# Two graph-attention layers on one core: gather buffers from a list of free ones, an earlier fetch at the change of layers, a moved transpose, the last tile by halves

## The chip, the cores and the metric

The kernel runs on one core of one Trainium2 chip. The metric is the device time of one execution in microseconds (us). The time before is the median of three runs, 1907.87 us (1905.23, 1907.87 and 1914.99).

## The reference

x is 3327 x 1024 in float32, adj is a symmetric 0/1 matrix with ones on its diagonal, in which an off-diagonal entry is set with a chance of about 0.0048. Cut to what matters:

```python
def layer0(x, adj, W, a_src, a_dst):          # 8 heads of 128
    h = (x @ W).reshape(C, H, D)
    e = leaky_relu(alpha_src[:, :, None] + alpha_dst[:, None, :], 0.2)
    attn = softmax(where(adj == 0, -inf, e), axis=-1)
    return einsum('hij,hjd->hid', attn, h)    # heads side by side

def layer1(x, adj, W, a1, a2):                # one head
    h = x @ W
    e = leaky_relu(h @ a1 + (h @ a2).T, 0.2)
    return relu(softmax(where(adj > 0, e, NEG), axis=1) @ h)

x = layernorm(x + layer0(x, adj, ...))
x = layernorm(x + layer1(x, adj, ...))
```

## The kernel before

The rows are cut into NT = 26 tiles of 128 (the last one has 127). A first stage projects x with layer 0's weights, one tile after the other, writes the projected rows to a table h0_d in DRAM, and works out for every tile the lists of its neighbours. It also sums layer 0's first half of sources for the first 13 tiles (the "early" ones). What is in question here comes after it, in the function `sparse`.

There a tile's neighbours are laid out in blocks. A tile of layer 1 ("Target") has blocks 0 to 4: four of 4 x 128 rows and a last one of 128 rows, the end. In layer 0 a late tile has the same five blocks, an early tile only 2, 3 and 4. For each block the function `gather` fetches the neighbours' rows from the table with indirect DMAs issued on POOL (L1034), four for a block, one for an end. A row of the table is 4.2 KB in layer 0 (h0_d) and 4.1 KB in layer 1 (y_d), so that a block is some 2.1 MB. The buffers are five for blocks (two named `near`, three `src`) and two for ends; they are taken round and round, a ring. A fetch goes out when the tenant before, five blocks back in the order of fetches, has been summed (`send`, L1320).

With a block in SBUF, `weights` works out its attention weights on DVE with a hand-over to ACT (layer 0: L1110, L1111, ACT's copy L1113, and e, L1115; layer 1: L1246, L1247, L1249), and `sums` multiplies it by PE into PSUM (L1146 in layer 0, L1258 in layer 1). `own` (L1080 on, L1224 on) adds the tile's own row. What is left of an item, its `finish`, is a generator that is advanced a step at a time while the following items run:

- Layer 0: the denominators (DVE met L1168, PE den L1169); dividing and adding x (L1172 to L1178); layer norm (L218 to L225) and two score products (L1185); three exponentials on ACT (L1190 to L1192, the last is `grow`) and the store of the row tile into y_d (L1193); last a transpose of `grow` on PE (L1197), its copy to a line on ACT (L1199) and the store of that line (L1200).
- Layer 1: transposing the sum z (L197, L200), multiplying it with layer 1's weights (L1290, 2 x 8 matmuls), ReLU and residual (L1293), layer norm, store (L1301).

The order of the instructions on every engine is the order in which the Python code emits them; nothing reorders them afterwards. `rest(i, n)` says how: before the first block of item i (n = 0) and after each block (n = 1 on) it advances the finishes of earlier items by the plan of the item's kind. In a pair such as (2, 1) the first number is an item two back, the second the item before. The plan of a layer 0 item with five blocks is

```python
len(Target.blocks): ((2,), (1,), (1,), (1,), (1,), (1,)),
```

so the last step of a finish (L1197, L1199, L1200) is emitted ahead of the first block's sums of the item two later, right after the exponentials of L1190 to L1192 and ahead of `own`.

Where the layers change, layer 1's gathers read y_d. Blocks 0 and 1 need only the first 13 tiles of it (`ready`, L1209), blocks 2 to 4 all 26. The list of fetches therefore goes, with A, B, C for targets 0, 1, 2: A0 A1 B0 B1, then A2 A3 A4 B2 B3 B4, then C0 and so on in order. The last item of layer 0 is finished in one go there (L1353), its row tile is stored, and A2 can be fetched.

Of the kernel before, what the change touches and what calls it, by code (L numbers as in the profile page):

```python
# [13 lines left out]
AF = mybir.ActivationFunctionType  # L14
OP = mybir.AluOpType
# [4 lines left out]
P = 128  # L20
SLOPE = 0.2
EPS = 1e-5
# [4 lines left out]
def kernel(  # L27
# [28 lines left out]
    nc = tc.nc  # L56
    N, D = x.shape
    H, DH = a0_src.shape
    NT = (N + P - 1) // P
# [4 lines left out]
    HALF = 512  # L64
    CT = 4
# [5 lines left out]
    EB = 4  # L71
    NB = NG * EB + 1
    WD = NP // 8
    HW0 = D + 2 * H
    HW = D + 4
# [6 lines left out]
    HB = EB // 2  # L82
# [31 lines left out]
    h0_d = scratch.tile([NP, HP], F32, name="h0_d")  # L114
    y_d = scratch.tile([NP, HP], F32, name="y_d")
# [19 lines left out]
    near = [const.tile([P, NG, HG], F32, name=f"near{b}") for b in range(HB)]  # L135
# [37 lines left out]
    class Phase:  # L173
# [16 lines left out]
        def sbuf(self, tag, shape, bufs, name=None, dt=F32):  # L190
            return self.pool.tile(shape, dt, tag=tag, name=name or tag, bufs=bufs)
# [322 lines left out]
    with ExitStack() as own, tc.manual_schedule():  # L514
        ph = Phase(own, "proj", {"A": 2, "T": 1})
# [243 lines left out]
        for n in range(4):  # L759
            half = slice(n % 2 * HALF, (n % 2 + 1) * HALF)  # L760
# [62 lines left out]
        for g in range(NG):  # L823
            nc.vector.memset(tri[g * GT : (g + 1) * GT, g * GT : (g + 1) * GT], 1.0)
        nc.gpsimd.affine_select(
            out=tri, in_=tri, pattern=[[1, P]], compare_op=OP.is_ge, fill=0.0, base=0, channel_multiplier=-1
# [7 lines left out]
            out=tri, in_=tri, pattern=[[1, P]], compare_op=OP.is_ge, fill=0.0, base=0, channel_multiplier=-1  # L834
# [35 lines left out]
        for t in range(3, NT):  # L870
# [3 lines left out]
            if t == 12:  # L874
                n, own_a = NT - 1, pool.tile([P, NT], I32, bufs=1, name="own")
# [95 lines left out]
    def sparse(own):  # L971
        ph = Phase(own, "sparse", {"A": 4, "S": 2, "T": 1, "E": 1})
        pool, bank, sbuf = ph.pool, ph.bank, ph.sbuf
        NS = 5
        srcs = near + [pool.tile([P, NG, HG], F32, bufs=1, name=f"src{n}") for n in range(HB, NS)]
        ends = [pool.tile([P, 1, HG], F32, bufs=1, name=f"end{n}") for n in range(2)]
# [46 lines left out]
        listed = {}  # L1023
        reach = {THR: nc.gpsimd.to_reg(THR - 1), NP: nc.gpsimd.to_reg(NP - 1)}
        stored = set()
        taken = [[(0, b) for b in range(HB)], []]

        def gather(table, w, t, b):
            end, n = b == EB, THR if b < HB else NP
            ring = ends if end else srcs  # L1030
            s = ring[len(taken[end]) % len(ring)]
            taken[end].append(None)
            for g in range(NG if b < EB else 1):
                nc.gpsimd.indirect_dma_start(  # L1034
                    out=s[:, g, :w], out_offset=None, in_=table[:n, :],
                    in_offset=bass.IndirectOffsetOnAxis(ap=idx[:, t, b * NG + g : b * NG + g + 1], axis=0),
                    bounds_check=reach[n], oob_is_err=False,
                )
            return s

        def get_edges(t):
            listed[t] = sbuf("re", [P, NB, H], 3)
# [14 lines left out]
        class Layer0:  # L1057


            def __init__(self, t, n):  # L1060
                self.t, self.n, self.src, self.made = t, n, {}, {}
                self.blocks = tuple(range(HB if t < EARLY else 0, EB + 1))

            def ready(self, b):
# [33 lines left out]
                self.acc = [bank("A", [P, 4, DH], "acc") for _ in range(2)]  # L1098

            def fetch(self, b):  # L1100
                self.src[b] = gather(h0_d, HW0, self.t, b)

            def weights(self, b):

# [97 lines left out]
        class Target:  # L1202
# [1 line left out]
            blocks = tuple(range(EB + 1))  # L1204

            def __init__(self, t, n):
                self.t, self.n, self.src, self.made = t, n, {}, {}

            def ready(self, b):  # L1209
                return stored.issuperset(range(NTH if b < HB else NT))  # L1210
# [20 lines left out]
                nc.vector.tensor_tensor(es[:, :1], es[:, 1:], loop[:, t : t + 1], OP.mult)  # L1231

            def fetch(self, b):
                self.src[b] = gather(y_d, HW, self.t, b)

            def begin(self):
                self.acc = {c: bank("A", [P, CUTS[1]], "acc1") for c in (2, 0, 1)}
# [42 lines left out]
            def finish(self):  # L1280

                t, z, res = self.t, self.z, self.res
                xT = sbuf("xT", [P, KT, P], 2)
                yield from ph.transposed(xT, z, (0, 1))
                o = sbuf("z", [P, D], 3, "o")
                for g in range(2):
                    half = slice(g * HALF, (g + 1) * HALF)
                    acc = bank("S", [P, HALF], "mm")
                    for k in range(KT):
                        nc.tensor.matmul(acc, xT[:, k, :], wt1[:, k, half], start=k == 0, stop=k == KT - 1)  # L1290
                        if k in (1, 3, 5):
                            yield
                    nc.vector.scalar_tensor_tensor(o[:, half], acc, 0.0, res[:, half], op0=OP.max, op1=OP.add)  # L1293
                    if g == 1:
                        ahead.append(self.settle(o))
                    yield

            def settle(self, o):
                yield from ph.norm_steps([o])
                for r in pieces(self.t):  # L1300
                    nc.sync.dma_start(out[at(self.t, r), :], o[r])  # L1301

        def pipeline(items, fetches):

            left, sums_of, sent = [], set(), [0]
            plans = {
                len(Target.blocks): ((2,), (1,), (1,), (1,), (1,), (1,)),
                len(Target.blocks) - HB: ((2,), (1, 1), (1, 1), (1,)),
                Target: ((2,), (2, 1), (2, 1), (1, 1), (1, 1), (1,)),
            }  # L1310

            def rest(i, n):
                it = items[i] if i < len(items) else items[-1]
                plan = plans[Target] if isinstance(it, Target) else plans[len(it.blocks)]
                for who in plan[n]:
                    k = i - who
                    if 0 <= k < len(left):
                        next(left[k], None)

            def send():  # L1320
                while sent[0] < len(fetches):
                    i, b = fetches[sent[0]]
                    end = b == EB
                    ring = len(ends) if end else NS
                    held = taken[end][-ring:]
                    if len(held) == ring and held[0] not in sums_of or not items[i].ready(b):
                        return
                    items[i].fetch(b)
                    taken[end][-1] = (i, b)
                    sent[0] += 1  # L1330

            def get(i):
                if i < len(items) and isinstance(items[i], Layer0):
                    get_edges(items[i].t)

            get(0)
            items[0].prepare()
            for av, a in zip(avs, (a1_src, a1_dst)):
                spread(av, a)
            for b in range(HB):  # L1340
                items[0].src[b] = near[b]
            send()
            items[0].weights(items[0].blocks[0])
            for i, it in enumerate(items):
                after = items[i + 1] if i + 1 < len(items) else None
                turn = isinstance(it, Target) and isinstance(items[i - 1], Layer0)
                it.begin()
                nb = len(it.blocks)
                for j, b in enumerate(it.blocks):
                    if j == 0 and i:  # L1350
                        items[i - 1].close()
                        if turn:
                            for _ in range(5):  # L1353
                                next(left[i - 1])
                            send()
                            it.weights(b)
                        rest(i, 0)
                    if j == 0:
                        get(i + 1)
                    if j == nb // 2 and after:  # L1360
                        after.prepare()
                    if j == 0:
                        it.own()
                    if j + 1 < nb:
                        it.weights(it.blocks[j + 1])
                    elif after and type(after) is type(it):
                        after.weights(after.blocks[0])
                    it.sums(b)
                    sums_of.add((i, b))
                    send()  # L1370
                    rest(i, j + 1)
                    run(ahead, 2 if i == 0 else 1)
                left.append(it.finish())
            items[-1].close()
            for i in (len(items), len(items) + 1):
                for n in range(EB + 2):
                    rest(i, n)
                    run(ahead)
            run(ahead, -1)
# [163 lines left out]
```

## Time and profile before

| | us |
|---|---|
| median of three runs | 1907.87 |
| profiled execution | 1802.07 |
| its span, first to last instruction | 1800.40 |
| PE busy | 1549.4 (86% of the span) |
| DVE busy | 1185.0 (66%) |
| ACT busy | 515.0 (29%) |
| POOL busy | 1110.4 (62%) |
| mean granted PE clock | 0.908 |

The profile is of one execution, which took 105.8 us less than the median of the runs; shares and places are read from it, and times in it stand against 1802.07. L12 is line 12 of the kernel before. "A <- B" in a list of waits is an engine that stood idle before A until B released it. In the timeline the columns are start (us), length (us), engine, line, operation and tiles, number of instructions merged, and in brackets the idle time before and what ended it.

### The profile page before, as it was taken

The numbers are of one execution on the slowest core, as the hardware profiler recorded it, in microseconds if no ns is written. First come the engines' busy times: TensorE is split into PE (matmuls) and PEld (weight loads), VectorE is DVE, ScalarE is ACT, GpSimd is POOL, SyncE is SP. The second block draws the span as 40 slices with busy tenths as digits, with TensorE's granted clock in tenths as the row PEclk, the third lists the DMA queues.
The fourth block names the chain that finished last, engine by engine and source line by source line (L and its number), as shares of the span: only waits on it lengthen the run. The fifth ranks groups of instructions, "written<-read, shape, count | busy, mean of one in ns | idle before, by whom it ended". The sixth has DMA issues, their size and how long they took to land.

```text
span 1800.4 us, 35590 instructions
## 1 busy us (share of the span) xinstructions
PE 1549.4 (86%) x13168; PEld 913.4 (51%) x13168; DVE 1185.0 (66%) x3261; ACT 515.0 (29%) x1519; POOL 1110.4 (62%) x1580
## 2 busy tenths in 40 slices
PE   8899989999994677676767667599999999999998
PEld 4566656666663555554545545244444444444443
DVE  5799999898865877777777776434444444444443
ACT  5666665554431222222222222111111111111110
POOL 4533337677745766666666665577777777777650
PEclk9999999999996777877787777799999999999999
DMA  7455859999879999999999999899999999999990
GB/s 191 91 117 125 159 110 300 266 298 287 277 260 338 412 412 402 394 393 402 395 390 399 398 396 327 331 390 407 403 389 402 398 407 407 371 400 396 386 379 35
DMA packets 187161, 586.89 MB, mean 326 GB/s; under 512 B 36610, under 2 KB 46620, under 8 KB 186978
## 3 DMA queue, kind: packets, MB, share of 16 engines
q0 software_dynamic: 131056, 457.74, 71.2%
q1 hardware_dynamic: 55922, 126.78, 19.1%
q8 instruction: 107, 1.75, 0.4%
q14 instruction: 76, 0.62, 0.1%
HBM read 587.80 MB, written 51.23 MB: 355 GB/s over the span
## 4 chain that ended last, share of the span: by engine, by line
PE 57%; DVE 19%; DMA 12%; issue 6%; ACT 4%; POOL 2%; DVEq 0%; SPq 0%; ACTq 0%; POOLq 0%
PE mm L1290 21%; PE acc L1258 13%; PE mm L546 11%; DMA src<-h_d,idx 6%; PE acc L1146 3%; PE part L671 2%; DVE e L1115 2%; PE tr L197 2%; DMA near<-h_d,idx 2%; ACT junk L350 1%; DMA end<-h_d,idx 1%; DVE pr L1185 1%; DVE top L309 1%; DVE y L1178 1%; DMA wt<-in_L_gnn_W_dram 1%
## 5 line engine op out<-in xcount | busy, mean ns | idle before, releaser
L546 PE MATMUL mm<-wt,xT 128*128 128x347 f32 (+1 forms) x1248 | 410.6, 470 | 4.2 <-DMA wt<-in_L_gnn_W_dram 4.2
L1290 PE MATMUL mm<-wt,xT 128*128 128x512 f32 x832 | 387.6, 604 | 0.0
L1034 POOL DMA_INDIRECT src<-y_d,idx x248 | 253.0, 1020 | 120.8 <-PE acc L1258 35.5
L546 PEld LDWEIGHTS mm<-wt,xT 128*128 128x128 f32 x1248 | 226.1, 192 | 121.9 <-issue 23.6
L1034 POOL DMA_INDIRECT src<-h_d,idx x184 | 194.6, 1058 | 113.3 <-issue 24.9
L1290 PEld LDWEIGHTS mm<-wt,xT 128*128 128x128 f32 x832 | 149.7, 189 | 198.6 <-issue 193.6
L1034 POOL DMA_INDIRECT near<-y_d,idx x168 | 170.3, 1013 | 67.6 <-PE acc L1258 28.5
L1293 DVE SCALAR_TENSOR_TENSOR o<-mm,y 128x512 f32<-128x512 f32 x52 | 35.9, 691 | 234.3 <-PE mm L1290 234.3
L1034 POOL DMA_INDIRECT near<-h_d,idx x120 | 130.2, 1085 | 74.2 <-PE acc L1146 29.5
L1115 DVE TENSOR_TENSOR e<-oh,way 128x1024 f32<-128x1024 f32 x104 | 126.9, 1221 | 59.4 <-ACT w L1113 51.2
L1258 PE MATMUL acc<-src,es 128*32 128x341 f32 x1488 | 122.8, 464 | 21.2 <-DVE es L1249 21.2
L200 ACT ACTIVATE xT<-tr 128x512 f32<-128x512 f32 x104 | 62.3, 600 | 249.1 <-PE tr L197 249.1
L1146 PE MATMUL acc<-src,e 128*32 128x128 f32 x2944 | 132.3, 354 | 0.2
L1146 PEld LDWEIGHTS acc<-src,e 128*32 128x32 f32 x2944 | 111.6, 145 | 31.1 <-issue 17.5
L1272 ACT ACTIVATE z<-y,ri 128x342 f32<-128x342 f32 (+1 forms) x78 | 39.5, 569 | 294.9 <-DVE ri L1268 294.9
L1113 ACT ACTIVATE w<-way 128x32 f32<-128x32 f32 x104 | 20.2, 194 | 320.6 <-DVE way L1111 314.1
L1146 PE MATMUL acc<-near,e 128*32 128x128 f32 x2048 | 94.7, 362 | 16.2 <-DVE e L1115 16.2
L1146 PEld LDWEIGHTS acc<-near,e 128*32 128x32 f32 x2048 | 79.3, 147 | 40.8 <-issue 24.6
L641 POOL DMA_INDIRECT near<-h_d,idx x76 | 82.6, 1087 | 26.0 <-issue 17.9
L1197 PE MATMUL tr<-ident,grow 128*128 128x128 f32 x26 | 11.4, 437 | 91.5 <-ACT grow L1192 91.5
L1258 PEld LDWEIGHTS acc<-src,es 128*32 128x32 f32 x1488 | 42.7, 111 | 90.8 <-issue 44.2
L350 ACT ACTIVATE junk<-ad 128x1664 uint8<-128x1664 uint8 x52 | 82.5, 1586 | 5.0 <-POOL ad L339 3.8
(241 smaller groups left out, 2588.7 us busy)
## 6 DMA issues: line engine op xcount, KB each, us to landing
h_d<-ht SPq DMA_DIRECT2D x26, 520.0 KB
own<-h_d SPq DMA_DIRECT2D x26, 520.0 KB
y_d<-y SPq DMA_DIRECT2D x26, 514.0 KB
y<-y_d SPq DMA_DIRECT2D x26, 514.0 KB
x<-in_x_dram SPq DMA_DIRECT2D x25, 512.0 KB
y<-in_x_dram SPq DMA_DIRECT2D x25, 512.0 KB
out_dram<-o SPq DMA_DIRECT2D x25, 512.0 KB
ad<-in_adj_dram POOLq DMA_DIRECT2D x25, 415.9 KB
```

Of the source, the lines that this page charges most:

```text
L197: nc.tensor.transpose(tr[:, k, :], src[:, (4 * g + k) * P : (4 * g + k + 1) * P], ident)
L200: nc.scalar.activation(part, tr, AF.Copy)
L350: nc.scalar.activation(junk, ad[:, n * THR : (n + 1) * THR], AF.Copy, accum_out=self.d[:, n : n + 1])
L546: nc.tensor.matmul(acc, xT[t][:, k, :], wt[:, k, CUTS0[c] : CUTS0[c + 1]], start=k == 0, stop=k == KT - 1)
L641: nc.gpsimd.indirect_dma_start(out=src[n % 3][:, g, :], out_offset=None, in_=h0_d[:THR, :], in_offset=bass.IndirectOffsetOnAxis(ap=idx[:, ...
L671: nc.tensor.matmul(acc[g * GT : (g + 1) * GT, h // 4, h % 4, :], e[:, g, h, :], vals[:, g, h, :], start=b == 0 and h % 4 == 0, stop=b == H ...
L1034: nc.gpsimd.indirect_dma_start(out=s[:, g, :w], out_offset=None, in_=table[:n, :], in_offset=bass.IndirectOffsetOnAxis(ap=idx[:, t, b * NG ...
L1115: nc.vector.tensor_tensor(e, oh.unsqueeze(2).to_broadcast([P, ng, H, wide]), wp.unsqueeze(3).to_broadcast([P, ng, H, wide]), OP.mult,)
L1146: nc.tensor.matmul(self.acc[h // 4][g * GT : (g + 1) * GT, h % 4, :], e[:, g, h, :], rowsof[:, g, h, :], start=first and h % 4 == 0, stop= ...
L1258: nc.tensor.matmul(self.acc[c][to, :m], es[:, g, :], s[:, g, CUTS[c] : CUTS[c + 1]], start=b == 0, stop=b == EB,)
L1272: nc.scalar.activation(z[:, cut], self.res[:, cut], AF.Copy, scale=ri[:, 1:2])
L1290: nc.tensor.matmul(acc, xT[:, k, :], wt1[:, k, half], start=k == 0, stop=k == KT - 1)
```

## The change

It has four parts:

- The ring is replaced by two lists of free buffers (`free`): a fetch takes the first free one, and a block's buffer goes to the end of the list when the block has been summed.
- The list of fetches puts C0 behind B1: A0 A1 B0 B1 C0, then A2 A3 A4 B2 B3 B4 C1 and so on. All five buffers are then taken ahead of the change of layers, and A2 takes the one that A0 leaves.
- In the last tile of layer 1 each half's bn_stats follows its L1293 at once, the normalising is done in two halves, and each half is stored by itself, the first by SP, the second by ACT.
- The plans of layer 0 change: the step of the item two back moves from n = 0 to n = 1, so that L1197, L1199 and L1200 are emitted behind the first block's sums (on ACT behind es L1082, own L1093 and w L1113 of block 1; on SP behind the load L1043).

```diff
-        taken = [[(0, b) for b in range(HB)], []]
+        free = [deque(range(HB, NS)), deque(range(len(ends)))]
 
         def gather(table, w, t, b):
             end, n = b == EB, THR if b < HB else NP
-            ring = ends if end else srcs
-            s = ring[len(taken[end]) % len(ring)]
-            taken[end].append(None)
+            k = free[end].popleft()
+            s = (ends if end else srcs)[k]
...
-            return s
+            return s, k
...
                     nc.vector.scalar_tensor_tensor(o[:, half], acc, 0.0, res[:, half], op0=OP.max, op1=OP.add)
+                    if t == NT - 1:
+                        if g == 0:
+                            self.st = sbuf("st", [P, CT, 2, 6], 2)[:, 0]
+                        nc.vector.bn_stats(self.st[:, g, :], o[:, half])
                     if g == 1:
                         ahead.append(self.settle(o))
                     yield
 
             def settle(self, o):
-                yield from ph.norm_steps([o])
-                for r in pieces(self.t):
-                    nc.sync.dma_start(out[at(self.t, r), :], o[r])
+                if self.t < NT - 1:
+                    yield from ph.norm_steps([o])
+                    for r in pieces(self.t):
+                        nc.sync.dma_start(out[at(self.t, r), :], o[r])
+                    return
+                mv, sg = sbuf("mv", [P, CT, 2], 2)[:, 0], sbuf("sg", [P, 2, CT], 2)
+                nc.vector.bn_aggr(mv, self.st.rearrange("p a b -> p (a b)"))
+                nc.vector.tensor_scalar(sg[:, 0, :1], mv[:, 1:2], EPS, None, op0=OP.add)
+                nc.scalar.activation(sg[:, 0, :1], sg[:, 0, :1], AF.Sqrt)
+                yield
+                nc.vector.reciprocal(sg[:, 1, :1], sg[:, 0, :1])
+                for g in range(2):
+                    half = slice(g * HALF, (g + 1) * HALF)
+                    nc.vector.tensor_scalar(
+                        o[:, half], o[:, half], mv[:, 0:1], sg[:, 1, :1], op0=OP.subtract, op1=OP.mult
+                    )
+                    for r in pieces(self.t):
+                        (nc.sync, nc.scalar)[g].dma_start(out[at(self.t, r), half], o[r, half])
...
             plans = {
-                len(Target.blocks): ((2,), (1,), (1,), (1,), (1,), (1,)),
-                len(Target.blocks) - HB: ((2,), (1, 1), (1, 1), (1,)),
+                len(Target.blocks): ((), (2, 1), (1,), (1,), (1,), (1,)),
+                len(Target.blocks) - HB: ((), (2, 1, 1), (1, 1), (1,)),
                 Target: ((2,), (2, 1), (2, 1), (1, 1), (1, 1), (1,)),
             }
...
                     i, b = fetches[sent[0]]
-                    end = b == EB
-                    ring = len(ends) if end else NS
-                    held = taken[end][-ring:]
-                    if len(held) == ring and held[0] not in sums_of or not items[i].ready(b):
+                    if not free[b == EB] or not items[i].ready(b):
                         return
                     items[i].fetch(b)
-                    taken[end][-1] = (i, b)
                     sent[0] += 1
...
                     it.sums(b)
-                    sums_of.add((i, b))
+                    free[b == EB].append(it.buf.pop(b))
                     send()
...
-        for c in (range(HB), range(HB, EB + 1)):
-            fetches += [(NT + i, b) for i in range(2) for b in c]
-        fetches += [(NT + i, b) for i in range(2, NT) for b in Target.blocks]
+        ahead_of = [(NT + i, b) for i in range(3) for b in range(HB)][: NS]
+        fetches += ahead_of
+        fetches += [(NT + i, b) for i in range(NT) for b in Target.blocks if (NT + i, b) not in ahead_of]
```

More of the change, by code (lines that the diff above doesn't have):

```diff
@@ L1060, in __init__ @@
             def __init__(self, t, n):
-                self.t, self.n, self.src, self.made = t, n, {}, {}
+                self.t, self.n, self.src, self.made, self.buf = t, n, {}, {}, {}
                 self.blocks = tuple(range(HB if t < EARLY else 0, EB + 1))
@@ L1100, in fetch @@
             def fetch(self, b):
-                self.src[b] = gather(h0_d, HW0, self.t, b)
+                self.src[b], self.buf[b] = gather(h0_d, HW0, self.t, b)
             def weights(self, b):
@@ L1206, in __init__ @@
             def __init__(self, t, n):
-                self.t, self.n, self.src, self.made = t, n, {}, {}
+                self.t, self.n, self.src, self.made, self.buf = t, n, {}, {}, {}
             def ready(self, b):
@@ L1233, in fetch @@
             def fetch(self, b):
-                self.src[b] = gather(y_d, HW, self.t, b)
+                self.src[b], self.buf[b] = gather(y_d, HW, self.t, b)
             def begin(self):
@@ L1298, in settle @@
             def settle(self, o):
-                yield from ph.norm_steps([o])
-                for r in pieces(self.t):
-                    nc.sync.dma_start(out[at(self.t, r), :], o[r])
+                if self.t < NT - 1:
[16 more added lines that the diff above has]
+                        (nc.sync, nc.scalar)[g].dma_start(out[at(self.t, r), half], o[r, half])
         def pipeline(items, fetches):
-            left, sums_of, sent = [], set(), [0]
+            left, sent = [], [0]
             plans = {
-                len(Target.blocks): ((2,), (1,), (1,), (1,), (1,), (1,)),
-                len(Target.blocks) - HB: ((2,), (1, 1), (1, 1), (1,)),
+                len(Target.blocks): ((), (2, 1), (1,), (1,), (1,), (1,)),
+                len(Target.blocks) - HB: ((), (2, 1, 1), (1, 1), (1,)),
                 Target: ((2,), (2, 1), (2, 1), (1, 1), (1, 1), (1,)),
@@ L1340, in pipeline @@
             for b in range(HB):
-                items[0].src[b] = near[b]
+                items[0].src[b], items[0].buf[b] = near[b], b
             send()
```

## The prediction

> **What bounds the kernel now.** I read the slices of the span first, then the waits of DVE and PE inside layer 0, the stage table, and the timeline of one change of items and of the change of layers. Times are from the span's start.
>
> The slices (40 of 45 us each), PE's busy tenths and the bytes moved:
>
> ```profile
> PE   8899989999994677676767667599999999999998
> ...
> GB/s 191 91 117 125 159 110 300 266 298 287 277 260 338 412 412 402 394 393 402 395 390 399 398 396 327 331 390 407 403 389 402 398 407 407 371 400 396 386 379 35
> ```
>
> Three stages show: the projections to about 555 us; layer 0's late sums, 560 to 1135, with PE at six or seven tenths; layer 1 from 1135, with PE at nine tenths or more. The two slices at 327 and 331 GB/s are the change of layers. In layer 1 the stage table gives PE 50.00 of 50 us busy from 1200 to 1750 at clock 1.00, one target per 24.57 us (two L1266 on DVE, 1721.11 and 1745.73, are one target apart). So there PE alone is the bound, and only idle PE time at the change of layers can be won.
>
> Layer 0 is the question. DVE's waits from 620 to 1075 (total us, times, longest):
>
> ```profile
> DVE e L1115 <- ACT w L1113: 42.2, 82, 2.3
> DVE es L1083 <- ACT es L1082: 28.4, 21, 1.4
> ...
> DVE way L1110 <- DMA end<-h_d,idx: 2.4, 1, 2.4
> DVE way L1110 <- DMA near<-h_d,idx: 1.0, 1, 1.0
> DVE way L1110 <- DMA src<-h_d,idx: 0.8, 1, 0.8
> ```
>
> DVE waited 4.2 us for gathered rows in 455 us. It is not short of data: it is a serial chain with hand-overs to ACT. PE waits behind it, in the same window:
>
> ```profile
> PE tr L1197 <- ACT grow L1192: 78.2, 21, 5.8
> ```
>
> The stage table (length, PE, PEld, DVE, ACT, POOL busy, PE clock, DMA share, GB/s):
>
> ```profile
> 600.00:625.00 25.00, 15.36 (x234) 11.21 (x233) 18.76 (x51) 6.84 (x21) 18.76 (x18) 0.86 1.02 413
> ...
> 620.00:1075.00 455.00, 325.11 (x4759) 244.65 (x4751) 355.25 (x928) 115.22 (x335) 296.22 (x278) 0.76 1.01 398
> ```
>
> DVE is busy 355 of 455 us; its listed waits (89.5 us) and the gaps between instructions are the rest. The DMA moves 398 GB/s where the first stretch shows 413, sustained (411 to 413) up to 675 us. A share near 1 doesn't prove saturation: at 1170 to 1175 it is 1.00 with 357 GB/s. So DVE sets layer 0's pace with the DMA 3.5% behind it.
>
> One change of items:
>
> ```profile
> 868.28 0.08 DVE L1185 DVE_READ_ACCUMULATOR pr<-y,wa 128x1 f32 x1
> 868.40 0.20 ACT L1190 ACTIVATE y<-sd 128x1 f32<-128x1 f32 x1 [1.13 <-DVE pr L1185]
> ...
> 868.60 0.19 ACT L1192 ACTIVATE grow<-sd 128x1 f32<-128x1 f32 x1
> ...
> 868.84 0.47 PE L1197 MATMUL tr<-ident,grow 128*128 128x128 f32 x1 [4.00 <-ACT grow L1192]
> ...
> 869.35 0.27 ACT L1199 ACTIVATE line<-tr 1x128 f32<-1x128 f32 x1 [0.56 <-PE tr L1197]
> 869.52 0.19 ACT L1082 ACTIVATE es<-sd 128x8 f32<-128x8 f32 x1
> ...
> 869.75 0.17 DVE L1083 TENSOR_TENSOR es<-es,own 128x8 f32<-128x8 f32 x1 [1.38 <-ACT es L1082]
> ```
>
> DVE stands still from 868.36 to 869.75. ACT's es needs nothing of L1197, but it queues behind the copy L1199, which waits for PE's transpose. PE too had waited 4.00 us for grow before the next block's sums.
>
> **What the skill says.** The Trainium skill, page "PSUM — Partial Sum Buffer", section "Engine vs sequencer instructions", says that ScalarE's queue is strictly first in, first out and that matmuls keep program order; the trace agrees: ACT idles 0.56 us before L1199, with es ready behind it. Page "DMA: Bandwidth & Descriptors", section "Queues, rings and completion order": the 16 DMA engines alternate between the queues that have work, a packet at a time. The trace agrees as far as it goes: own<-h_d, issued by SP at 1096.10, was awaited until 1105.7 while gathers ran. Page "TensorE: Matmul & The Clock Gate", section "What's actually happening": after an idle window PE runs at half clock. Here a block's 24 sums take 3.65 us after 10.04 us of idleness, otherwise 1.93.
>
> **The change, part by part.**
>
> *The plans.* In layer 0 the step L1197, L1199, L1200 of the item two back moves from ahead of a new item's first block sums to just after them. PE's order becomes 64 sums records, tr, den; ACT's becomes grow, es, own, w of block 1, line, w of block 2; on SP the re load L1043 passes ahead of the row store L1200. No instruction is added. The price: L1190 to L1192 follow each other at 0.1 us, so es would start about 868.70, end at 868.89, and DVE's L1083 follow 0.03 later as it does now, at 868.93: **0.82 us** saved per item, of DVE's own chain. PE's sums can start when e (L1115) is ready, 867.22, instead of 869.24: 2 us earlier, which frees their gather buffer as much earlier. From 675 to 1075 some 18 items change: 18 x 0.82 = 14.8 us. The limit is the DMA: 181.17 MB from 620 to 1075 need 439.7 us at 412 GB/s, so at most 15.3 us. Both limits lie together, and work with two near limits gets neither in full; I take two thirds, **10 us** (bounds 0 and 14.8). The items before 675 already run at 411 to 413: nothing. At 1078.67 and 1100.52 the DMA has room (308 to 337 GB/s) and POOL waits 6.26 us for those very sums, so up to 2 us each; I take **2 us** in all (0 to 4), as the second item then waits for own<-h_d until 1105.7.
>
> What waits behind the moved step: on ACT, w of block 2, and for it DVE's e. With sums from 867.3, 3.64 us at half clock, tr 0.47 and line 0.27, the copy ends near 871.7; w of block 2 (now at 874.95) would be due at 874.1. It is covered by 2.4 us.
>
> *The free list and the early block.* In layer 0 buffers come back in the order they are taken, so the list equals the ring. At the change (targets A, B, C of layer 1, blocks 0 to 4) the present timeline is:
>
> ```profile
> 1139.70 1.00 POOL L1034 DMA_INDIRECT src<-y_d,idx  x1 [9.04 <-DMA row_d<-line]
> ...
> 1150.07 3.65 PE L1258 MATMUL acc<-src,es 128*32 128x341 f32 x24 [10.04 <-DVE es L1249]
> ...
> 1156.04 1.93 PE L1258 MATMUL acc<-src,es 128*32 128x341 f32 x24 [2.32 <-DVE es L1249]
> ...
> 1173.44 1.93 PE L1258 MATMUL acc<-near,es 128*32 128x341 f32 x24 [2.68 <-DVE es L1249]
> ```
>
> A0, A1, B0, B1 are fetched early (POOL 1109.91 to 1130.66). A2 waits for the last row store, issued near 1134.1, and starts at 1139.70; PE has done A1 at 1140.03, idles 10.04 us for A2, 2.32 for A3, later 2.68 for B3. Now C0 takes the fifth buffer: four gathers of 1.0 + 0.3 us on POOL, 1130.96 to 1135.9, in POOL's idle 9.04 us, 2.1 MB in the DMA's slack (188 GB/s from 1135 to 1140). A2 must then also wait for A0's sums, done at 1137.9: no loss. But its start hangs on the row store, which now shares the DMA with C0: 5.3 us from issue as it is, up to 9.4 as for the store of 1100.40 (gather at 1109.91). So A2 and A3 come 0 to 4 us later; I take 2.5. B2 takes A2's buffer, freed at 1153.7 + 2.5, and is issued by 1161.4, some 6 us before PE comes to it: covered. B3 no longer waits for B0's buffer: it takes A3's, is issued by 1166.6 (1167.2 now), lands 4 to 5 us later as A2 did, and PE comes to it at 1170.8 + 2.5: 2.68 us won. C0 itself is needed at 1184, when PE is the bound: hidden before and after, worth nothing. Sum **about 0** (-2.7 to +2.5).
>
> *The last tile.* After the last L1293 (1791.99 to 1792.68) stand two bn_stats (1.27 us), aggregate to reciprocal, and 0.81 us of normalising, then the store until 1800.4. One bn_stats moves under PE's last 6 us: 0.6 won. The first half's store starts 0.4 us earlier and the last one carries half the bytes; one more store goes on ACT's queue, idle by then. I take **1 us** (0 to 2).
>
> Sum: 10 + 2 + 0 + 1 = **13 us**. The profiled execution, 1802.07 us (span 1800.40), would become 1789. The median of the runs shown, 1907.87, is 105.8 us above it; no view says where. I carry the 13 us over: **1894.9 us**. If the slower runs had PE at a lower clock, layer 1 would only be more PE-bound, and the gain stands; if they had slower DMA, it shrinks to the first rival.
>
> **The rivals.** *The DMA is the real limit of layer 0* (0.32). For it: 396 to 402 GB/s in most stretches, near 412, and chain pieces of 13 us from a gather's issue to its landing. Against: DVE's 4.2 us of waiting for data. DVE's 0.82 us per item then turns into waits for gathers (L1110); what is left is 1 us at the end and 2 to 4 near the change of layers: 1904, not told from no change.
>
> *ACT's copy holds DVE* (0.07, slower). L1199 now waits for the new item's sums as well as the transpose, ahead of w of block 2. It decides from the point where sums end more than 2.4 us later than worked out. At 1.5 us of DVE standstill over 26 items, 39 us less the 13 won: 1934. Against it: PE is free at 864.84 and e is ready 2 us before the present start.
>
> *The early block alone decides* (0.05): PE may have slack at the moved step for a reason that the trace hides, and only the change of layers moves, 2.5 us either way, 1905 to 1910. For it: nothing but A2's wait is long there; against: DVE's wait at L1083 is on its serial chain.
>
> **How the numbers follow.** DVE-paced layer 0, 0.56: 1894.9, own range 1882 to 1900. The measurement tells about 0.5%, 9.5 us, from no change. Low end: 14.8 + 4 + 2 + 2.7 = 23.5 us, 1884.4, and 4 us for the spread of medians (runs reach from 1905.23 to 1914.99): 1880. High end: no gain in layer 0 and the change of layers 2.5 us late, 1910, less its rarer part: 1909. Chances: faster 0.56, same 0.32 + 0.05 = 0.37, slower 0.07.
>
> **What would show it.** Right: DVE's wait at L1083 falls from 1.36 to about 0.5 us each; PE's wait at L1197 vanishes; 620 to 1075's work shows over 405 GB/s and layer 0 ends some 10 us earlier; the B3 wait is gone, A2's stays near 10 us. Wrong: DVE's waits for L1110's gathers grow from 4 us to over 12 (the DMA), or e L1115 waits on w for more than 42 us (the copy), or A2's idle time passes 14 us.

## The result, and the profile after

| the pair of record | us, median of 6 runs (lowest to highest) |
|---|---|
| before | 1914.3 (1905.23 to 1923.32) |
| after | 1879.26 (1876.39 to 1883.75) |
| ratio | 0.983, 95% interval 0.980 to 0.986 |

The change made the kernel 35 us faster here, not 13. One fact is needed to read every number below: the same kernels also ran on other chips, and the kernel before took about 1916 us on the chip of the first experiments but 1802 and 1803 us on the two chips of the later ones. The profile of before that the prediction read (1802.07 us) looks like one from a chip of the second kind, target by target, and so the 105.8 us between it and the runs were no scatter. I call the kinds "the 1910 kind" (the pair of record is of it) and "the 1802 kind". **On the 1802 kind the change brings nothing**: 1802.22 against 1802.15 us, ratio 0.9999 (0.9987 to 1.0012). What makes the two kinds is not shown: no chip was seen in both, and what ran beside the kernel on each chip isn't known.

The new lines are numbered one lower than before (es on DVE is L1082, rows' weights L1109, e L1114, sums L1145, tr L1196). The slices of the profiled execution after (1883.75 us, span 1882.0 us):

```profile
PE   8899899999995777778677767499999999999998
...
GB/s 184 90 136 117 149 173 261 230 273 248 272 245 348 390 403 372 374 380 389 380 394 395 363 366 328 267 369 389 385 379 373 389 390 385 369 385 377 369 355 34
```

The slices are 47 us long here, not 45. The stages are the same, but no slice of layer 0 stays at the 412 GB/s that opened it in the profile shown before. In layer 1 PE is full from slice to slice as it was, but a target takes 25.3 us instead of 24.6; that is so before the change too on this kind of chip.

The kernel before was profiled again on a chip of the 1910 kind (span 1909.3 us), which is what the profile after has to be held against. Stage by stage, from the starts of the first sums of layer 0's late part (L1146), of layer 1 (L1258) and of the last matmul (L1290), in us:

| | up to layer 0's late sums | layer 0 | layer 1 | tail | span |
|---|---|---|---|---|---|
| 1910 kind, before | 584.6 | 628.0 | 687.7 | 9.0 | 1909.3 |
| 1910 kind, after | 587.2 | 604.8 | 681.6 | 8.4 | 1882.0 |
| 1802 kind, before (prediction's profile) | 564.1 | 570.6 | 656.7 | 9.0 | 1800.4 |
| 1802 kind, before but for the tail (e3 below) | 564.0 | 572.6 | 659.1 | 8.4 | 1804.1 |
| 1802 kind, after | 557.5 | 569.4 | 660.2 | 8.4 | 1795.5 |

Of the 27.3 us between the first two rows, 23.2 lie in layer 0, 6.1 in layer 1, 0.6 in the tail, and 2.6 go the other way in a part that the change doesn't touch. (The execution profiled after was the longest of its six, and single profiles of the same plans differ by up to 3 us in layer 0: e2 below, with those of before, takes 631.0 us there, and e1, with the new ones, 603.6.) On the 1802 kind layer 0 takes 570.6 and 572.6 us with the plans of before and 569.4, 569.1 and 571.0 with the new ones (e6, e5, e10), so it wins some 2 us; layer 1 loses 1 to 3.5. The last row's 6.5 us ahead of layer 0 are again in a part that the change leaves alone: over nine profiles of this kind it varied from 556 to 565 us.

What DVE waited for from 620 to 1075 on the 1910 kind, first before, then after (total us, times, longest):

```profile
DVE es L1083 <- ACT es L1082: 33.0, 13, 6.7
...
DVE es L1083 <- issue: 23.4, 4, 7.4
DVE es L1083 <- ACT line L1199: 9.3, 2, 5.7
...
DVE ri L1172 <- PE den L1169: 6.9, 8, 2.5
```

```profile
DVE ri L1171 <- PE den L1168: 25.9, 6, 5.1
DVE ri L1171 <- PE tr L1196: 12.5, 3, 4.7
...
DVE ri L1171 <- remote: 10.1, 2, 7.1
DVE es L1082 <- ACT y L1189: 3.9, 7, 0.6
```

Before, es cost DVE 65.7 us for 20 items, 3.3 us each, not the 1.36 us of the prediction's profile. After, all waits at es make 11.2 us for 20 items, 0.56 each. But DVE now stands at ri (48.5 us; 12.4 before) until PE comes to den. What is left of the gain in this window is 65.7 + 12.4 - 11.2 - 48.5 = 18.4 us for 20 items, 0.92 us an item, and 26 items make about the 23 us of the stage table. (DVE's other waits hardly move: those at e go from 45.7 to 46.5 us, those at met from 0 to 3.9. As a check, DVE does 333.1 us of work in the window instead of 320.6, a factor of 1.039, and 628.0 by 604.8 is 1.038.) Waits for gathered rows (L1109) are 0.3 us in all.

The same window of after on the 1802 kind:

```profile
DVE e L1114 <- ACT w L1112: 46.3, 85, 2.2
DVE es L1082 <- ACT es L1081: 11.1, 20, 0.6
DVE ri L1171 <- PE den L1168: 8.0, 12, 0.7
DVE way L1109 <- issue: 5.2, 3, 2.4
DVE way L1109 <- DMA src<-h_d,idx: 4.4, 6, 1.7
DVE way L1109 <- DMA near<-h_d,idx: 4.1, 2, 2.1
DVE way L1109 <- DMA end<-h_d,idx: 4.0, 2, 2.5
...
DVE es L1082 <- ACT grow L1191: 1.1, 2, 0.6
```

Here es fell as predicted, from 28.4 to 12.2 us in all (11.1 and 1.1), which is 16.2 us won. The rows' weights L1109 rose from 4.2 to 17.7 us (12.5 of it put down to the DMA, 5.2 to issue) and ri from 6.8 to 8.0: 14.7 us given back. e waits longer for w (42.2 to 46.3), but no longer for PE, and all its waits together stay at 47 us. What is left is under 2 us of 455. The DMA moved 398 GB/s in this window, as before.

### The profile page after: what moved, and what is told of

Read it like the earlier page. It is cut to its first block, busy times and chain, and to the rows that moved or that the text cites. A ratio compares the mean times of both kernels' runs of the same rounds, so it can differ in the third digit from the quotient of the medians.

```text
span 1882.0 us, 35565 instructions
## 1 busy us (share of the span) xinstructions
PE 1637.2 (87%) x13168; PEld 934.7 (50%) x13168; DVE 1184.3 (63%) x3262; ACT 514.0 (27%) x1519; POOL 1105.5 (59%) x1580
## 3 DMA queue, kind: packets, MB, share of 16 engines
q8 instruction: 107, 1.75, 0.4%
## 4 chain that ended last, share of the span: by engine, by line
PE 64%; DVE 14%; issue 9%; ACT 5%; DMA 5%; POOL 2%; another core or an unknown queue 0%; SPq 0%; DVEq 0%; ACTq 0%; POOLq 0%
PE mm L1289 20%; PE acc L1257 14%; PE mm L546 10%; PE acc L1145 9%; PE part L671 3%; PE acc L1126 2%; PE tr L197 2%; PE acc L1134 2%; ACT junk L350 1%; ACT own L1092 1%; DVE e L1114 1%; DMA wt<-in_L_gnn_W_dram 1%; DMA src<-h_d,idx 1%; DVE top L309 1%; DVE y L1177 1%
## 5 line engine op out<-in xcount | busy, mean ns | idle before, releaser
L1033 POOL DMA_INDIRECT src<-y_d,idx x256 | 258.8, 1011 | 145.4 <-issue 56.6
L1033 POOL DMA_INDIRECT src<-h_d,idx x184 | 200.9, 1092 | 123.3 <-PE den L1155 34.4
L1145 PE MATMUL acc<-src,e 128*32 128x128 f32 x2944 | 164.9, 335 | 50.8 <-issue 49.4
L1033 POOL DMA_INDIRECT near<-y_d,idx x160 | 160.8, 1005 | 79.0 <-issue 32.6
L1145 PEld LDWEIGHTS acc<-src,e 128*32 128x32 f32 x2944 | 116.0, 134 | 111.8 <-issue 92.0
L1114 DVE TENSOR_TENSOR e<-oh,way 128x1024 f32<-128x1024 f32 x104 | 127.1, 1222 | 61.2 <-ACT w L1112 39.7
L1257 PE MATMUL acc<-src,es 128*32 128x342 f32 (+1 forms) x1536 | 138.5, 464 | 24.6 <-DVE es L1248 22.0
L1145 PE MATMUL acc<-near,e 128*32 128x128 f32 x2048 | 112.5, 339 | 48.9 <-issue 35.8
L1145 PEld LDWEIGHTS acc<-near,e 128*32 128x32 f32 x2048 | 81.3, 136 | 90.6 <-issue 77.3
L1257 PEld LDWEIGHTS acc<-src,es 128*32 128x32 f32 x1536 | 50.4, 111 | 101.6 <-issue 54.4
L1257 PE MATMUL acc<-near,es 128*32 128x342 f32 (+1 forms) x960 | 85.5, 455 | 3.9 <-DVE z L1274 1.7
```

What stands on the lines that cost most here:

```text
L1033: nc.gpsimd.indirect_dma_start(out=s[:, g, :w], out_offset=None, in_=table[:n, :], in_offset=bass.IndirectOffsetOnAxis(ap=idx[:, t, b * NG ...
L1114: nc.vector.tensor_tensor(e, oh.unsqueeze(2).to_broadcast([P, ng, H, wide]), wp.unsqueeze(3).to_broadcast([P, ng, H, wide]), OP.mult,)
L1145: nc.tensor.matmul(self.acc[h // 4][g * GT : (g + 1) * GT, h % 4, :], e[:, g, h, :], rowsof[:, g, h, :], start=first and h % 4 == 0, stop= ...
L1257: nc.tensor.matmul(self.acc[c][to, :m], es[:, g, :], s[:, g, CUTS[c] : CUTS[c + 1]], start=b == 0, stop=b == EB,)
```

## Experiments

The theories on record: A, DVE's hand-over to ACT paces layer 0; B, PE itself is late in the longer executions, by stops for "issue" (waits for nothing that the profile shows); C, the DMA bounds layer 0. The theories L, C (of the early C0), D to G are in the expectations. Ratios are to the kernel before on the same chip.

### First set: a chip of the 1910 kind (before 1916.42 us)

**e0_before**, no edit.

> The kernel before, unchanged, for a profile of an execution that takes as long as the medians do. Theory A (DVE's chain of hand-overs sets layer 0's pace): about 1914 us; DVE's wait for es at L1083 is 1.36 us an item again, and DVE has few other waits. Theory B (in the longer executions PE itself is late: it stops for issue between matmuls, 73 us of it in layer 0 of the changed kernel's profile): the 106 us over the first profile show as PE waiting for issue, and DVE then waits for PE (ri L1172 for den) in layer 0. Theory C (the DMA is the bound): DVE waits for gathered rows at L1110, well over the 4.2 us of the first profile.

Measured: 1911.0 us (one run), and PE does stop for issue. The timeline of before on this chip, PE, ACT and DVE at a change of items:

```profile
707.77 1.84 PE L1146 MATMUL acc<-near,e 128*32 128x128 f32 x45
709.98 0.47 PE L1146 MATMUL acc<-near,e 128*32 128x128 f32 x5 [0.38 <-issue]
710.71 0.46 PE L1146 MATMUL acc<-near,e 128*32 128x128 f32 x4 [0.26 <-issue]
711.44 0.45 PE L1146 MATMUL acc<-near,e 128*32 128x128 f32 x4 [0.27 <-issue]
...
717.17 0.32 PE L1197 MATMUL tr<-ident,grow 128*128 128x128 f32 x1
...
717.53 0.27 ACT L1199 ACTIVATE line<-tr 1x128 f32<-1x128 f32 x1 [5.92 <-PE den L1139]
717.71 0.19 ACT L1082 ACTIVATE es<-sd 128x8 f32<-128x8 f32 x1
717.93 0.17 DVE L1083 TENSOR_TENSOR es<-es,own 128x8 f32<-128x8 f32 x1 [6.74 <-ACT es L1082]
```

After 45 matmuls at full rate PE gets through four or five every 0.73 us. So its old sums end late, the transpose is late, ACT's line copy stands 5.92 us, es queues behind it, and DVE stands 6.74 us. The same coupling through ACT's queue that cost 1.36 us on the other kind costs up to 7 here. The stops sum to 51.8 us in 123 places from 620 to 1075 before, and to 65.2 us in 140 after: the change doesn't remove them. So B has its stops, but before the change they reach DVE at es, by way of ACT's queue, and hardly at ri (12.4 us).

**e1_plans**, the plans alone:

```diff
-                len(Target.blocks): ((2,), (1,), (1,), (1,), (1,), (1,)),
-                len(Target.blocks) - HB: ((2,), (1, 1), (1, 1), (1,)),
+                len(Target.blocks): ((), (2, 1), (1,), (1,), (1,), (1,)),
+                len(Target.blocks) - HB: ((), (2, 1, 1), (1, 1), (1,)),
```

> Only the two plans of layer 0 changed: L1197, L1199 and L1200 behind the first block's sums. Theory A: 12 to 16 us faster than before (0.7 to 0.9%), as DVE's es comes 0.82 us earlier in 26 items. Theory B: 25 to 32 us faster (1.3 to 1.7%), nearly all of what the whole change gave, as PE loses a wait of 3.5 us an item that its own stops no longer leave room for. Theory C: under 5 us.

Measured: 1888.0 us, ratio 0.984 (0.980 to 0.989). Layer 0 takes 603.6 us instead of 628.0, layer 1 690.5. This is the size that B named. By the times the plans give 28 us, and e2 below 5: together about the 35 of the pair. The plans alone give after's layer 0.

**e4_es_first**, the order of before, with ACT's es issued ahead of the line copy:

```diff
+            def early(self):
+                self.es = sbuf("es0", [P, H], 2)
+                nc.scalar.activation(self.es, sd0[:, self.t, 0, :], AF.Exp, scale=1 - SLOPE)
...
+                        if isinstance(it, Layer0):
+                            it.early()
                         rest(i, 0)
```

> The kernel before with one ACT instruction moved: es (L1082) is emitted ahead of the line copy (L1199), PE's transpose stays ahead of the first block's sums. It gives DVE the 0.82 us an item and leaves PE its wait for grow. Theory A: as fast as the moved plans, 12 to 16 us faster than before. Theory B: 0 to 6 us faster, and the moved plans win much more. Theory C: nothing.

Measured: 1894.36 us, ratio 0.988 (0.984 to 0.992); layer 0 takes 615.9 us. This leaves tr ahead of PE's sums and takes away only the queueing on ACT. Most of the plans' gain comes from there: 22 of 28 us by the times, 12.1 of 24.4 us by layer 0 of the profiles, each of one execution (the intervals of e1 and e4 overlap). DVE's waits at es fall to 11.1 us as in after, and those at ri rise from 12.4 to 43.8 us:

```profile
DVE ri L1174 <- PE den L1171: 43.8, 10, 5.9
```

So 31 of the 55 us won at es come back at ri, although tr is in its old place. Neither theory had the size (A 12 to 16 us, B 0 to 6): A is right on the place, and the late PE of B makes the loss there larger than A counted.

**e2_free_c0**, the free lists and the early C0, plans and tail as before (their diff lines above):

> Only the lists of free buffers and the early fetch of C0, with the plans and the last tile as before. Theory A and B: within 3 us of before. Rival (the change of layers is what the whole change won by): 15 us or more faster.

Measured: 1910.97 us, ratio 0.998 (0.996 to 1.000), layer 1 681.6 us against 687.7. So 6 us in layer 1 by the stages, 5 by the times: more than the 3 us that A and B allowed, but not the 15 or more that the rival wanted. From the end block's sums of target B to those of C it takes 27.5 us, where it took 33.4 with the ring.

### Second set: a chip of the 1802 kind (before 1802.15 us)

**e3_tail**, the last tile by halves alone (its diff lines above):

> The kernel before with the last tile by halves alone. The prediction priced it at 1 us (0 to 2). The theory that layer 0's moved step makes the result expects 1 us here, a ratio of 0.9995 to the kernel before, not told from 1; in the profile 7.8 us from the start of the last ReLU on DVE to the end, where the kernel before takes 8.4. The rival: the missing part of the result (35 us were measured, the plans alone gave 30) lies in the tail; then 3 to 5 us less, a ratio near 0.998.

Measured: 1802.71 us, ratio 0.9999 (0.9985 to 1.0013). The profile has a tail of 8.4 us instead of 9.0. Too small to be told by the times.

**e6_after**, the changed kernel on this chip:

> The changed kernel again, beside the others on one chip. If the parts add up, the plans 30 us, list and early C0 4 us, tail 1 us: a ratio of 0.982 (0.980 to 0.985). A second profile of it should have PE's stops for issue in layer 0 (55 to 76 us in the four longer executions) if they belong to executions of this length, and a target of layer 1 should take 25.3 us; an execution without the stops should take about 1790 us and 24.6 us a target.

Measured: 1802.22 us, ratio 0.9999. The expectation was for 0.982: it failed, this chip being of the other kind. PE has no rows of short stops here (what stands under issue is 12 waits of up to 3.3 us ahead of an item's first sums), and a target takes 24.6 us. The mechanism of the prediction is there nevertheless; the timeline of a change of items:

```profile
860.87 0.19 ACT L1191 ACTIVATE grow<-sd 128x1 f32<-128x1 f32 x1
860.96 0.19 ACT L1081 ACTIVATE es<-sd 128x8 f32<-128x8 f32 x1
...
861.19 0.17 DVE L1082 TENSOR_TENSOR es<-es,own 128x8 f32<-128x8 f32 x1 [0.55 <-ACT es L1081]
...
864.28 0.25 ACT L1198 ACTIVATE line<-tr 1x128 f32<-1x128 f32 x1
```

es follows grow at once, DVE waits 0.55 us, and the line copy comes 3.3 us later, in nobody's way.

**e5_free_oldorder**, the changed kernel with the old list of fetches:

```diff
-        ahead_of = [(NT + i, b) for i in range(3) for b in range(HB)][: NS]
-        fetches += ahead_of
-        fetches += [(NT + i, b) for i in range(NT) for b in Target.blocks if (NT + i, b) not in ahead_of]
+        for c in (range(HB), range(HB, EB + 1)):
+            fetches += [(NT + i, b) for i in range(2) for b in c]
+        fetches += [(NT + i, b) for i in range(2, NT) for b in Target.blocks]
```

> The changed kernel with the fetch list of before (A0 A1 B0 B1 A2 A3 A4 B2 B3 B4 C0), so with the free lists but without the early C0. Theory L, the list gives the 6 us of layer 1, as B3 no longer waits for B0's buffer: B3's wait (2.5 to 3.1 us) is gone, target B to C takes 27 to 30 us, and the ratio is that of the changed kernel. Theory C, the early C0 gives them, as fewer gathers are issued back to back behind A2: B to C stays at 33 to 37 us although B3's wait is gone, and the kernel takes 4 to 6 us more than the changed one. Either way layer 0 is as in the changed kernel, 600 to 607 us from its first late sums to layer 1's first.

Measured: 1797.53 us, ratio 0.9971 (0.9961 to 0.9981), so 4.7 us *under* the changed kernel; layer 1 takes 656.0 us against 660.2. Neither theory had that: on this kind the early C0 costs. First PE without it; then PE, POOL and, over 5 us, the stretch 1150 to 1155 with it (the columns of that row are those of the prediction's stage table):

```profile
1149.23 3.65 PE L1257 MATMUL acc<-src,es 128*32 128x341 f32 x24 [11.86 <-DVE es L1248]
1154.48 1.93 PE L1257 MATMUL acc<-src,es 128*32 128x341 f32 x24 [1.60 <-DVE es L1248]
```

```profile
1146.40 3.65 PE L1257 MATMUL acc<-src,es 128*32 128x341 f32 x24 [13.21 <-DVE es L1248]
1151.57 3.64 PE L1257 MATMUL acc<-src,es 128*32 128x341 f32 x24 [1.52 <-DVE es L1248]
...
1163.70 1.93 PE L1257 MATMUL acc<-src,es 128*32 128x341 f32 x24 [1.00 <-DVE es L1248]
```

```profile
1135.44 1.00 POOL L1033 DMA_INDIRECT src<-y_d,idx  x1 [5.94 <-DMA row_d<-line]
...
1150.30 1.00 POOL L1033 DMA_INDIRECT src<-y_d,idx  x1 [3.40 <-PE acc L1257]
```

```profile
1150.00:1155.00 5.00, 3.48 (x28) 0.99 (x24) 2.67 (x9) 0.00 (x0) 3.79 (x4) 0.50 0.57 168
```

A2 is waited for 1.35 us longer: its first gather, released by the last row's store, starts 4.5 us after A1's sums begin, not 3.0 (the DMA carries C0 at 403 GB/s from 1130 to 1135, where it had 327 and then 123 without). The block at 1163.70 is waited for another 1.00 us, since its gather could only start when A2 had been summed: POOL stood 3.40 us and the DMA fell to 168 GB/s. A3's sums take 3.64 us instead of 1.93 and make up the other 1.71 of 4.2 us, but this can't be laid on C0: e9 below, with the ring and the old list, has it too.

```profile
1148.15 3.64 PE L1259 MATMUL acc<-src,es 128*32 128x341 f32 x24 [1.52 <-DVE es L1250]
```

The two waits come again in e8 (early C0: 13.17 and 1.72 us) against e10 (without: 11.31 and none). So 2.4 to 3.6 us are what the profiles show for the early C0; the times say 4.7. On the 1910 kind the DMA moved only 205, 109 and 47 GB/s in the three stretches of 5 us from 1185 on of after: C0 was long in.

**e7_half_rows**, the kernel before with part of the rows of layer 0's late gathers left out:

```diff
+        less = {THR: nc.gpsimd.to_reg(THR // 2 - 1), NP: nc.gpsimd.to_reg(THR + (NP - THR) // 2 - 1)}
...
-                    bounds_check=reach[n], oob_is_err=False,
+                    bounds_check=(less if table is h0_d and b < EB and len(taken[0]) > 20 else reach)[n], oob_is_err=False,
```

> The kernel before, with the bounds of layer 0's late gathers lowered so that about half of the rows are left out of them (same instructions, about half of the bytes); layer 1 is unchanged. It asks whether PE's stops for issue between matmuls in layer 0 come from the load on the DMA. Theory F, they do: PE's idle time before layer 0's matmuls that is put down to issue falls from 55 to 76 us to under 20 us in 480 us, DVE's wait at es (3.2 us an item) falls to about 1.4, and layer 0 gets 30 us or more shorter, while layer 1 keeps its 25.3 us a target. Theory G, they don't come from the load: they stay at 50 us or more, DVE's wait at es stays near 3 us, and layer 0 changes by less than 15 us, although the data come sooner.

Measured: 1798.04 us (one run). The chip was not of the kind that has the stops, so F and G stay apart. But layer 0 takes 562.4 us with 279 GB/s in the window of 620 to 1075, where e3 on the same chip took 572.6 with 397: with the old plans, 30% less data brings 8 to 10 us of 571 to 573. DVE's chain is the pace then: it has no wait for rows left, and its wait at es stays at 29.3 us.

### Third set and the last run: another chip of the 1802 kind (before 1803.05, then 1801.66 us)

**e8_after_half**, the same cut in the changed kernel (counted from the 19th block on), and **e9_half_again**, the cut in the kernel before:

> The changed kernel, with about half of the rows left out of layer 0's late gathers (same instructions; layer 1 unchanged). On the chip where the kernel before takes about 1802 us: Theory D, the rows took the gain there (DVE's wait at es fell from 28.4 to 11.1 us, its waits for rows at L1109 rose from 4.2 to 17.7): without that load DVE waits under 3 us for rows and layer 0 takes 545 to 552 us, against 562.4 with the plans of before and half of the rows; about 1783 us in all. Rival E, something else on PE or DVE took it, as in the wait of PE's den for DVE's met (48 to 74 us): layer 0 takes 558 us or more, about 1795 in all. On the chip where it takes about 1910 us, PE's stops for issue (73 us in layer 0) fall under 20 us if the load on the DMA makes them, and layer 0 takes under 575 us instead of 604.8; else they stay at 50 us or more and it takes over 595 us.

> The kernel before, with half of the rows left out of layer 0's late gathers, on the same chip as the changed kernel with half of them. Where the kernel before takes about 1802 us: 560 to 565 us of layer 0 again, DVE's wait at es 29 us. Where it takes about 1910 us, Theory F (the load on the DMA makes PE's stops for issue): under 20 us of stops, 1.4 us of wait at es an item, layer 0 under 590 us instead of 628. Theory G (the stops have another origin): stops of 50 us or more, 3 us of wait at es, layer 0 over 610 us.

Measured: e8 1778.0 us, ratio 0.9865 (0.9845 to 0.9884), layer 0 545.6 us; e9 1795.52 us (one run), layer 0 562.4. DVE's waits in 620 to 1075, first of e8, then of e9:

```profile
DVE es L1085 <- ACT es L1084: 12.2, 22, 0.6
...
DVE way L1112 <- DMA src<-h_d,idx: 0.4, 1, 0.4
```

```profile
DVE es L1084 <- ACT es L1083: 30.7, 23, 1.4
```

With the load off the DMA the moved step brings 562.4 - 545.6 = 16.8 us in layer 0, 0.65 us for each of 26 items. With all rows it brings some 2 (570.6 and 572.6 against 569.1 to 571.0). Theory D holds: on this kind the rows took the gain, and with either limit alone out of the way the other stays: 562 us with fewer rows and the old plans, 569 to 571 with the new plans and all rows, 546 with both.

**e10_oldorder_again**, the kernel of e5:

> The changed kernel with the old list of fetches (no early C0), as run on the chip where the kernel before takes 1802 us (ratio 0.997 there, 4.7 us under the changed kernel). There again 0.997. Where the kernel before takes about 1910 us, Theory L (the free list gives the 6 us of layer 1 there): a ratio of 0.980 to 0.984, target B to C 26 to 30 us. Theory C (the early C0 gives them): 0.985 to 0.988, B to C 33 us or more.

Measured: 1797.05 us, ratio 0.9970 (0.9958 to 0.9982): 0.997 again. This version beats the kernel before on both chips of the 1802 kind, and the changed kernel on the one where both ran; on the 1910 kind it was not tried.

**e11_half_before**, e7's kernel again, for the stops:

> The kernel before, with half of the rows left out of layer 0's late gathers. Where the kernel before takes about 1910 us: Theory F (the load of the gathers makes PE's stops for issue), under 20 us of stops in layer 0, 1.4 us of wait at es an item, layer 0 under 590 us instead of 628. Theory G (the stops have another origin), stops of 50 us or more, 3 us of wait at es, layer 0 over 610 us. Where the kernel before takes about 1802 us: 562 us of layer 0 and about 1796 us a third time.

Measured: 1793.3 us, ratio 0.9955 (0.9940 to 0.9971), layer 0 560.7 us. The chip was of the 1802 kind once more, so what makes PE's stops stays open.

## Why the prediction was right, and where it was not

- **The sign, and the place, were right.** On both kinds DVE's wait at es falls to 0.55 us an item and PE's wait ahead of tr vanishes, as named. That the kernel got faster by a clear margin was luck in part: on the kind of chip whose profile was read, the same mechanism brings nothing in the times. Two signs that were named did not come: 620 to 1075 shows 398 and 383 GB/s, not over 405, and layer 0 is shorter by 23 or by some 2 us, not by 10.
- **The step that failed is the last one, carrying the sum over.** The profile and the runs were 105.8 us apart, and the 13 us were taken from one to the other: 1894.9 us, with 1880 as the low end, where 1879.26 came. Both halves of the sentence that did so fail: on the 1802 kind the first rival is right (DVE's wait for rows passes its mark of 12 us, 17.7), on the 1910 kind the gain is neither the same nor smaller but more than twice as large (35 us, 23 of them in layer 0).
- **Layer 0: 10 us, and 2 for its last two items (bounds 0 to 18.8); measured 23.2 (1910 kind) and some 2 (1802 kind).** The term had 0.82 us an item, 18 items, and two thirds for the DMA's limit. On the 1910 kind the net is 0.92 us an item (2.7 won at es, 1.8 given back at ri), and 23.2 us come out only if all 26 items take part. No limit of the DMA cuts it off there: DVE's waits for rows are 0.3 us, and the DMA went from 364 to 383 GB/s in the window. On the kind of chip that was profiled the near limit takes not a third of the gain but most of it (e8 and e9).
- **The cover of w held.** All waits of e together go from 45.7 to 46.5 us in the window on the 1910 kind and from 46.9 to 46.6 on the 1802 kind; the slower rival did not come. Its mark, more than 42 us of waiting for w, was too low to tell: 46.3 us stand there after, but 44.9 with the plans of before in e3.
- **What was missing: den.** DVE, no longer held at es, comes to ri before PE has come to den, which stands behind the new item's sums. The prediction gave PE's order but followed only the copy. On the 1910 kind, where PE is late, 36 of 54 us come back at ri; e4, with tr in its old place, loses 31 there, so it is not the moved tr that does most of it.
- **Change of layers: about 0, bounds 2.7 won to 2.5 lost; measured 6.1 won (1910 kind) and 1 to 3.5 lost (1802 kind).** B3's wait is gone on both, as named; A2's grew (9.62 to 11.57 and 10.04 to 13.21, under the mark of 14). The price of A2's and A3's lateness was 2.5 us; B2's wait (1.00 and 1.72 us in e6 and e8), called covered, was not in it. On the 1802 kind the early C0 costs 4.2 us of layer 1 by the stages (e6 against e5), against which the list wins 1 to 3 (656.7 and 659.1 to e5's 656.0). On the 1910 kind the ring's target C came 8 us late (33.4 instead of 25.3), with PE stopping up to 1.7 us at a time while POOL issued gather after gather; the list and the early C0 together take away 6 to 7.5 of the 8, and the share of each was not measured there. (The two L1266 that the prediction sets one target apart are 24.62 us apart, not 24.57; nothing hangs on it.)
- **The last tile: 1 us; measured 0.6** in the profile, nothing in the times.

The Trainium skill, page "Runtime: NRT & Kernel Launch", section "Instruction fetch mechanics", says that engines fetch their instructions by DMA in blocks of 16 KiB, and calls the cost mostly hidden. The trace has such a queue (107 packets, 1.75 MB), and stops of PE that begin after a full-rate stretch would fit a late block; that they come from there is not shown. The kept traces give no sign of it: there are 107 such packets on either kind, they take 1.02 us in the mean in e0 and 1.04 in the prediction's profile, and the 123 stops of e0's window stand against 35 packets in it.

## What to carry to other kernels

When a profile and the runs that it is to explain differ by more than their scatter, the first question is whether they are of the same machine: read shares from a profile, but don't size a gain by its waits and limits before that is settled. An instruction that waits for a slow engine in a strict queue makes everything behind it as late as that engine is; moving it behind the urgent one is worth more the later the slow engine runs. And a stall taken from the pacing engine pays only as far as the next limit, which a run with less data shows at once.

## What was not expected of the hardware

- The same program takes 1802 us on two chips and 1911 to 1916 on another: 6%, in every stage (564 to 585, 571 to 628, 657 to 688 us), at no lower PE clock (0.908 and 0.920).
- On the slower one, PE stops between short matmuls (128 x 128 by 32) for 0.3 to 1.1 us, four or five matmuls apart, 52 us in 455; with layer 1's longer ones the stops are 1.3 us in 500.
- A prefetch was in before the transfer that matters on one chip and in its way on another: with C0, the DMA was down to 109 GB/s just before A2's gathers on the 1910 kind, and still at 403 on the 1802 kind, where C0 cost 4.7 us.
